# A mixture-of-experts kernel on one core: its expert blocks planned in two steps in place of three

## The chip, the core and the metric

The kernel runs on one core of one Trainium2 chip. The metric is the device time of one execution in microseconds (us). The core's engines are called as in the profile: PE (TensorE, the matmuls; PEld its weight loads), DVE (VectorE), ACT (ScalarE), POOL (GpSimd) and SP (SyncE, which here issues DMAs).

## What is computed

The input is x of 4 batches x 512 tokens x 256 features, all in fp32. Two residual layers follow each other; the layer norms in front of them have no parameters.

```python
x = x + attention(layernorm(x))
x = x + moe(layernorm(x))

def attention(x):                       # linear attention, 16 heads of 16
    q = k = elu(heads(x @ Wqk + bqk))
    v, u = silu(x @ Wv + bv), silu(x @ Wu + bu)
    out = merge(q @ (k^T @ v))          # per head
    return (u * layernorm(out, g, b)) @ Wo + bo

def moe(x):                             # 8 experts, the best 2 of each token
    top_w, top_i = top_k(x @ gate, 2)
    top_w = softmax(top_w)
    h = silu(x @ w0[e]) * (x @ w1[e])   # 256 -> 512
    return sum(top_w[e] * (h @ w2[e]) for e in top_i)   # 512 -> 256
```

There are 2048 tokens and two experts for each, so 4096 rows of expert work.

## The kernel before, in words

**Attention.** `attention(b)` is a generator that handles one batch in 15 stages, one for each `yield`. The loop over `at` runs the four batches staggered: batch b begins at `at` = 4b, and in each turn every batch that is under way does one stage. Stage 9 forms x1 (the first residual, matmuls `ap`) and writes it to the DRAM buffer `y` with a DMA from ACT. Stage 10 makes the third layer norm, `hn` (even quarters on DVE at L236, odd ones on ACT at L232). Stages 11 to 14 transpose it (`hTp`), multiply by the gate (`lp`), find the two best experts and each row's place (`mask`, `pre`, matmuls `pos`, `idx`), and scatter the rows with eight indirect DMAs from POOL (L461) into the DRAM buffer `xg`. There each expert has a region of its own, filled in the order of the tokens. A row carries its routing weight and the number of its token.

**Plans.** The expert work is cut into blocks of 128 rows of one expert. How many full blocks each expert has is known on the chip alone, so `plan(n, b)` works out a table of n blocks there: it sums the counts so far with a matmul (`tot`), and some 22 small DVE instructions turn them into a first row and two weight offsets for each block. `tot_False` and its tiles belong to plans of full blocks, `tot_True` to the last plan, whose blocks (names that end in r) may be partly empty. A number of full blocks is sure whatever the routing is: all rows so far, divided by 128, less 7 for what may be left over in eight experts.

**Blocks.** A block passes four functions, and `advance(block)` moves a new block in and each one in flight on by one:

- `fetch`: SP reads the first row from the table (L552) and issues a DMA of 128 rows of `xg` into a tile `g` (L567). There are 8 such tiles. Before the first r block, `pads()` writes empty rows behind each region's end, with eight DMAs on SP (L476), since partly empty blocks read past it.
- `turn`: PE transposes `g` into `gp` (L578), ACT copies it (L581), and then ACT and DVE each copy one half of the expert's first weights from `hw_sb` into a staging slot (L587).
- `hidden`: 32 matmuls `hp` (L598), silu into `s` on ACT (L604), a product `it` on DVE (L606).
- `finish`: 8 matmuls `eo` on w2 (L615), a scaling into `ys` on DVE (L620), and an indirect DMA from POOL that adds the rows to DRAM (L624). The rows go to `y`, or straight to the output for blocks in the list `held`, which run last; ahead of the first of those POOL copies all of `y` to the output (L623).

**Order.** When batches 1, 2 and 3 have gone through their last stage (at = 19, 23, 27), a plan is made of the blocks that are sure by then and were not planned yet: 9, 8 and 8. The first nine follow in `ready` after two empty turns (`[None] * 2`), one block for each turn of the loop. Of the eight of batch 2, five follow in `ready` and three are held back (`HELD = 3`). After batch 3 a second, last plan has 14 r blocks; eleven follow in `ready` and three run only where routing is that uneven (`rare`, under `tc.If`). At the end run the held blocks, the eight of batch 3 first. So the order is 9 and 5 blocks, 11 r blocks, 8 and 3 held ones, 36 in all. The instructions of each engine then run in the order that the built program gives them, which is close to that of the source; engines wait for each other by semaphores.

Of the kernel before, what the change touches and what calls it, by code (L numbers as in the profile page):

```python
# [19 lines left out]
P = 128  # L20
# [5 lines left out]
def kernel(  # L26
# [30 lines left out]
    B, N, E = x.shape  # L57
    NE, _, M = w0.shape
# [4 lines left out]
    T = B * N  # L63
    TOPK = 2
    BLOCKS = T * TOPK // P + NE - 1
    USUAL = T * TOPK // P + NE // 2
    HELD = 3
    REG = T + P
    ROW = E + 4
    HW = 2 * EC * M  # L70
# [407 lines left out]
    def plan(n, b, last=False):  # L478

        tot = psum.tile([P, NE], F32, tag="a", name=f"tot_{b}_{last}")
        nc.tensor.matmul(tot, lhsT=ones, rhs=state["count"], start=True, stop=True)
        vec = [1, NE]

        def tmp(shape, what):
            return small.tile(shape, F32, tag=what, name=f"{what}_{b}_{last}", bufs=1)

        c = tmp(vec, "c")
        nc.vector.tensor_copy(c, tot[0:1, :])  # L490
        if last:

            state["pads"] = const.tile(vec, I32, name="pads_at")
            nc.vector.tensor_tensor(state["pads"], c, region[0:1], ALU.add)
            nc.vector.tensor_scalar(c, c, float(P - 1), None, ALU.add)
        full = [1, NE, T // P]
        over = tmp(full, "over")
        nc.vector.tensor_tensor(
            over, c.unsqueeze(2).to_broadcast(full), ends, ALU.is_ge
        )  # L500
        new = tmp(vec, "new")
        nc.vector.tensor_reduce(new, over, AX.X, ALU.add)
        nc.vector.tensor_tensor(new, new, done, ALU.subtract)

        sq = tmp([1, NE, NE], "sq")
        nc.vector.tensor_tensor(
            sq, new.unsqueeze(1).to_broadcast([1, NE, NE]), upto[0:1], ALU.mult
        )
        cum = tmp(vec, "cum")
        nc.vector.tensor_reduce(cum, sq, AX.X, ALU.add)  # L510
        cumex = tmp(vec, "cumex")
        nc.vector.tensor_tensor(cumex, cum, new, ALU.subtract)

        base = tmp(vec, "base")
        nc.vector.tensor_tensor(base, done, cumex, ALU.subtract)
        nc.vector.scalar_tensor_tensor(base, base, float(P), region[0:1], ALU.mult, ALU.add)
        nc.vector.tensor_tensor(
            step[:, 0 : NE - 1], base[:, 1:NE], base[:, 0 : NE - 1], ALU.subtract
        )

        grid = [1, n, NE]
        behind = tmp(grid, "behind")
        nc.vector.tensor_tensor(
            behind, ordinal[:, 0:n, :], cum.unsqueeze(1).to_broadcast(grid), ALU.is_ge
        )
        which = tmp([1, n], "which")
        nc.vector.tensor_reduce(which, behind, AX.X, ALU.add)
        nc.vector.tensor_tensor(
            behind, behind, step.unsqueeze(1).to_broadcast(grid), ALU.mult
        )  # L530
        first = tmp([1, n], "first")
        nc.vector.tensor_reduce(first, behind, AX.X, ALU.add)
        nc.vector.scalar_tensor_tensor(
            first, first, base[:, 0:1], rows[:, 0:n], ALU.add, ALU.add
        )
        table = const.tile([1, 3, n], I32, name=f"table_{b}_{last}")
        nc.vector.tensor_scalar(table[:, 0, :], first, float(NE * REG), None, ALU.min)
        nc.vector.tensor_scalar(table[:, 1, :], which, float(NE - 1), float(HW), ALU.min, ALU.mult)
        nc.vector.tensor_scalar(table[:, 2, :], which, float(NE - 1), float(OW), ALU.min, ALU.mult)
        if last:  # L540
            state["rest"] = const.tile([1, 1], I32, name="rest")
            nc.vector.tensor_copy(state["rest"], cum[:, NE - 1 : NE])
        else:
            taken = tmp(vec, "taken")
            nc.vector.tensor_scalar(taken, cumex, -1.0, float(n), ALU.mult, ALU.add)
            nc.vector.scalar_tensor_tensor(taken, taken, 0.0, new, ALU.max, ALU.min)
            nc.vector.tensor_tensor(done, done, taken, ALU.add)
        return [(f"{b}_{j}{'r' if last else ''}", b, table[0:1, :, j : j + 1]) for j in range(n)]
# [11 lines left out]
    def fetch(block):  # L560

        j, b, entry = block
        if j == f"{B - 1}_0r":
            pads()
        row = read(entry[:, 0, :], NE * REG, mybir.EngineType.SP)
        g = blk.tile([P, ROW], F32, tag="g", name=f"g_{j}", bufs=8)
        ins = nc.sync.dma_start(out=g, in_=xg[bass.ds(row, P), :])  # L567
        tc.declare_no_dep(ins.ins, group=f"after {b}", reason="rows of batches up to b")
        tc.add_to_no_dep_group("reads", ins.ins)
        return block, g  # L570

    def turn(block, g):


        j, b, entry = block
        ps = psum.tile([P, EC, P], F32, tag="a", name=f"gp_{j}")
        for c in range(EC):
            nc.tensor.transpose(ps[:, c, :], g[:, bass.ts(c, P)], ident)  # L578
        gT = arena[:, 8, bass.ts(state["turned"] % 4, E)].rearrange("p (c n) -> p c n", c=EC)
        state["turned"] += 1  # L580
        nc.scalar.copy(gT, ps)  # L581
        at = read(entry[:, 1, :], (NE - 1) * HW, mybir.EngineType.Activation, mybir.EngineType.DVE)
        w = []
        for i, copy in enumerate((nc.scalar.copy, nc.vector.tensor_copy)):
            w.append(staging[state["staged"] % 4])
            state["staged"] += 1
            copy(w[i], hw_sb[:, bass.ds(at + i * EC * M, EC * M)])  # L587
        return block, w, g, gT

    def hidden(block, w, g, gT):  # L590

        j = block[0]
        both = []
        for i in range(2):
            ps = psum.tile([P, MC, P], F32, tag="a", name=f"hp_{j}_{i}")
            for m in range(MC):
                for k in range(EC):
                    nc.tensor.matmul(  # L598
                        ps[:, m, :], lhsT=w[i][:, bass.ds(k * M + m * P, P)],
                        rhs=gT[:, k, :], start=(k == 0), stop=(k == EC - 1),  # L600
                    )
            both.append(ps)
        s = work.tile([P, MC, P], F32, tag="s", name=f"s_{j}")
        nc.scalar.activation(s, both[0], AF.Silu)  # L604
        it = work.tile([P, MC, P], F32, tag="ex", name=f"it_{j}", bufs=4)
        nc.vector.tensor_tensor(it, s, both[1], ALU.mult)  # L606
        return block, g, it
# [26 lines left out]
    fetched, turned, made, held = [], [], [], []  # L634

    def advance(block=None):


        if block is not None:
            fetched.append(fetch(block))  # L640
        if fetched and (len(fetched) > 1 or block is None):
            turned.append(turn(*fetched.pop(0)))
        if turned and (len(turned) > 1 or not fetched):
            made.append(hidden(*turned.pop(0)))
        if made and (len(made) > 1 or not turned):
            finish(*made.pop(0))
# [3 lines left out]
    STAGES = 15  # L650
    W2_AT = 9
    begin = [0, 4, 8, 12]
    running = [attention(b) for b in range(B)]
    ready, ran, routed = [], 0, []
    for at in range(max(begin) + STAGES + 1):
        for b in range(B):
            if begin[b] <= at < begin[b] + STAGES:
                next(running[b], None)
        if at == begin[B - 1] + W2_AT:
            load_w2()  # L660

        b = begin.index(at - STAGES) if at - STAGES in begin else 0
        if b > 0:
            sure = -(-(b + 1) * N * TOPK // P) - NE + 1
            blocks = plan(sure - ran, b)
            ran = sure
            if b < B - 2:
                ready += [None] * 2 + blocks
            elif b < B - 1:
                ready += blocks[:-HELD]  # L670
                held += blocks[-HELD:]
            else:
                rest = plan(BLOCKS - ran, b, last=True)
                ready += rest[: USUAL - ran]
                rare = rest[USUAL - ran :]
                held = blocks + held
        if ready:
            block = ready.pop(0)
            if block:
                advance(block)  # L680
    for block in ready + held:
        advance(block)
    while fetched or turned or made:
# [62 lines left out]
```

## Time and profile before

| | us |
|---|---|
| median of 3 runs (354.87 to 356.56) | 356.35 |
| the profiled execution's own time | 355.68 |
| its span, first to last instruction | 353.6 |
| PE busy in the span | 307.8 |
| DVE, ACT, POOL busy | 175.3, 135.3, 120.8 |
| mean granted TensorE clock, of 1 | 0.947 |

A row of a timeline has the start and the length in us, the engine with its line, the operation, output<-inputs by the program's names without buffer numbers, and how many instructions were merged; in brackets, how long the engine had been idle before and what ended that. In the page's slices each digit is the busy share of 8.84 us in tenths. Attention and routing of all batches fill the first 152 us or so, with the first blocks among them; from then on blocks run alone.

### The profile page before, as it was taken

Reading aid. Unit: us, or ns where it says so; the run is one execution under the profiler, and the core shown is the slowest. Engines: PE = TensorE matmul, PEld = TensorE weight load, DVE = VectorE, ACT = ScalarE, POOL = GpSimd, SP = SyncE. Lnnn points to the kernel's source line nnn. Section 1 sums busy time; section 2 is a strip of 40 time slices with the busy share of each in tenths; the row PEclk is TensorE's granted clock in tenths of the full one; section 3 lists DMA queues with packets and bytes.
Section 4 is the critical chain, followed back from the end, with each engine's and each line's share of the span. In section 5 each row is a group of like instructions: output and inputs, shape, how many; then the busy total and the mean of one; then the engine's idle time right before and its main releaser. Section 6 shows DMA issues by size and latency. Waiting matters only on the chain. (4 is left out here: it accounts for less than half of the span.)

```text
span 353.6 us, 6144 instructions
## 1 busy us (share of the span) xinstructions
PE 307.8 (87%) x2048; PEld 274.4 (78%) x2048; DVE 175.3 (50%) x620; ACT 135.3 (38%) x204; POOL 120.8 (34%) x143
## 2 busy tenths in 40 slices
PE   0899899899767639995999999999999999999950
PEld 0467586777666439994999999999999999999940
DVE  4855879896694775663532323323233232342210
ACT  1455728647313135622323324333243332433200
POOL 5410211406617137266323324243242321333331
PEclk9999999999896678999999999999999999999995
DMA  7999012051364452143236332332323353332221
GB/s 216 369 386 373 9 59 62 1 179 66 115 184 173 121 154 92 15 92 90 46 57 157 62 47 45 59 47 48 47 46 60 47 166 120 60 48 30 32 32 15
DMA packets 27871, 35.58 MB, mean 101 GB/s; under 512 B 2848, under 2 KB 22688, under 8 KB 27808
## 3 DMA queue, kind: packets, MB, share of 16 engines
q1 hardware_dynamic: 18960, 22.00, 19.8%
q0 software_dynamic: 6768, 11.08, 17.2%
q10 hardware_dynamic: 2112, 2.10, 1.9%
q8 instruction: 18, 0.29, 0.3%
q14 instruction: 13, 0.11, 0.1%
HBM read 22.89 MB, written 14.37 MB: 105 GB/s over the span
## 5 line engine op out<-in xcount | busy, mean ns | idle before, releaser
L598 PE MATMUL hp<-arena 128*128 128x128 f32 x800 | 96.3, 280 | 4.1 <-ACT arena L587 4.1
L598 PEld LDWEIGHTS hp<-arena 128*128 128x128 f32 x800 | 94.2, 197 | 4.4 <-ACT arena L587 4.3
L606 DVE TENSOR_TENSOR it<-s,hp 128x512 f32<-128x512 f32 x25 | 17.2, 688 | 61.4 <-PE hp L598 52.7
L461 POOL DMA_INDIRECT xg<-hn,idx_i x32 | 32.4, 1012 | 43.8 <-DVE rs L228 34.5
L615 PE MATMUL eo<-arena,it 128*128 x200 | 47.1, 379 | 0.0
L624 POOL DMA_INDIRECT y<-ys,g x14 | 24.6, 1757 | 50.2 <-DVE ys L620 37.9
L615 PEld LDWEIGHTS eo<-arena,it 128*128 128x128 f32 x200 | 36.2, 190 | 3.9
L587 ACT COPY arena<-hw_sb 128x1024 f32 x36 | 37.6, 1045 | 2.9 <-ACT arena L581 0.8
L581 ACT COPY arena<-gp 128x256 f32<-128x256 f32 x25 | 9.3, 373 | 72.3 <-PE gp L578 68.6
L624 POOL DMA_INDIRECT out_dram<-ys,g x11 | 17.5, 1590 | 38.7 <-issue 17.8
L253 POOL TENSOR_TENSOR x<-x,bo 128x256 f32<-128x256 f32 x16 | 12.8, 824 | 40.9 <-DVE arena L236 32.5
L587 DVE COPY arena<-hw_sb 128x1024 f32 x36 | 25.0, 695 | 1.8 <-issue 0.8
L360 PE MATMUL ap<-wo,arena 128*128 128x256 f32 x64 | 18.4, 452 | 8.5 <-DVE arena L352 4.5
L360 PEld LDWEIGHTS ap<-wo,arena 128*128 128x128 f32 x64 | 14.3, 230 | 12.1 <-issue 4.3
L620 DVE TENSOR_SCALAR ys<-eo,g 128x256 f32<-128x256 f32 x25 | 12.1, 482 | 22.5 <-PE eo L615 22.5
L604 ACT ACTIVATE s<-hp 128x512 f32<-128x512 f32 x25 | 14.9, 597 | 19.6 <-PE hp L598 10.5
L265 PE MATMUL qp<-arena,wqk 128*128 128x512 f32 x32 | 16.4, 662 | 0.2 <-ACT arena L258 0.2
L283 PE MATMUL vp<-wv,arena 128*128 128x256 f32 x64 | 14.5, 379 | 0.0
L214 DVE BATCH_NORM_STATS2 st<-x 128x6 f32<-128x256 f32 x32 | 12.7, 415 | 3.5 <-DMA x<-in_x_dram 3.4
L297 PE MATMUL up<-arena,wu 128*128 128x512 f32 x32 | 14.4, 592 | 0.0
L283 PEld LDWEIGHTS vp<-wv,arena 128*128 128x128 f32 x64 | 12.0, 190 | 2.4 <-issue 1.0
L244 PE MATMUL xTp<-ident,arena 128*128 128x128 f32 x32 | 5.2, 311 | 9.9 <-DVE arena L236 9.9
(275 smaller groups left out, 488.7 us busy)
## 6 DMA issues: line engine op xcount, KB each, us to landing
hw_sb<-in_w_dram SPq DMA_DIRECT2D x16, 512.0 KB
arena<-in_w_dram SPq DMA_DIRECT2D x8, 512.0 KB
g<-xg SPq DMA_DIRECT2D x25, 130.0 KB
x<-in_x_dram SPq DMA_DIRECT2D x4, 512.0 KB
y<-x ACTq DMA_DIRECT2D x4, 512.0 KB
xg<-empty SPq DMA_DIRECT2D x9, 130.0 KB
xg<-hn,idx_i POOLq DMA_INDIRECT x32
wqk<-in_wqk_dram SPq DMA_DIRECT2D x1, 256.0 KB
```

The source lines that it names most:

```text
L253: nc.gpsimd.tensor_tensor(xb[:, t, :], xb[:, t, :], bo_sb, ALU.add)
L265: nc.tensor.matmul(ps, lhsT=wqk_sb[:, k, bass.ts(c, P)], rhs=xT[:, k, :], start=(k == 0), stop=(k == EC - 1),)
L283: nc.tensor.matmul(ps[:, t - t0, :], lhsT=xT[:, k, bass.ts(t, P)], rhs=wv_sb[:, k, :], start=(k == 0), stop=(k == EC - 1),)
L297: nc.tensor.matmul(ps, lhsT=wu_sb[:, k, bass.ts(c, P)], rhs=xT[:, k, :], start=(k == 0), stop=(k == EC - 1),)
L360: nc.tensor.matmul(ps[:, t - t0, :], lhsT=yT[:, c, bass.ts(t, P)], rhs=wo_sb[:, c, :], start=(c == 0), stop=(c == EC - 1),)
L461: apart(nc.gpsimd.indirect_dma_start(out=xg[:, :], out_offset=bass.IndirectOffsetOnAxis(ap=idx_i[:, t, k : k + 1], axis=0), in_=hn[:, t, k ...
L587: copy(w[i], hw_sb[:, bass.ds(at + i * EC * M, EC * M)])
L598: nc.tensor.matmul(ps[:, m, :], lhsT=w[i][:, bass.ds(k * M + m * P, P)], rhs=gT[:, k, :], start=(k == 0), stop=(k == EC - 1),)
L604: nc.scalar.activation(s, both[0], AF.Silu)
L606: nc.vector.tensor_tensor(it, s, both[1], ALU.mult)
L615: nc.tensor.matmul(ps, lhsT=it[:, m, :], rhs=w2_sb[:, bass.ds(at + m * E, E)], start=(m == 0), stop=(m == MC - 1),)
L624: ins = nc.gpsimd.indirect_dma_start(out=whole[:, :] if full else y[:, :], out_offset=bass.IndirectOffsetOnAxis(ap=g[:, E + 1 : E + 2].bit ...
```

## The change

One plan is made when batch 1 is through (nine blocks, as before), and none when batch 2 is. After the loop, behind batch 3, one plan takes all sixteen full blocks that are sure by then, and the last plan has its 14 r blocks as before. All sixteen are in `held`: they run last and add to the output. The first nine follow after one empty turn, not two. The order is 9 blocks, 11 r blocks, 16 held ones, again 36. The two plans behind batch 3 also stand after that turn's `advance`, no longer ahead of it.

```diff
-    HELD = 3
+    EARLY = 2 * N * TOPK // P - NE + 1
+    SURE = T * TOPK // P - NE + 1
...
-    ready, ran, routed = [], 0, []
+    ready = []
...
-        b = begin.index(at - STAGES) if at - STAGES in begin else 0
-        if b > 0:
-            sure = -(-(b + 1) * N * TOPK // P) - NE + 1
-            blocks = plan(sure - ran, b)
-            ran = sure
-            if b < B - 2:
-                ready += [None] * 2 + blocks
-            elif b < B - 1:
-                ready += blocks[:-HELD]
-                held += blocks[-HELD:]
-            else:
-                rest = plan(BLOCKS - ran, b, last=True)
-                ready += rest[: USUAL - ran]
-                rare = rest[USUAL - ran :]
-                held = blocks + held
+        if at == begin[1] + STAGES:
+            ready += [None] * 1 + plan(EARLY, 1)
         if ready:
             block = ready.pop(0)
             if block:
                 advance(block)
+
+    held += plan(SURE - EARLY, B - 1)
+    rest = plan(BLOCKS - SURE, B - 1, last=True)
+    ready += rest[: USUAL - SURE]
+    rare = rest[USUAL - SURE :]
     for block in ready + held:
         advance(block)
```

`EARLY` is 9 and `SURE` is 25.

## Prediction

> **What bounds the kernel now.** I read the page first (busy time, the slices, the chain that ended last), then the timeline of PE, then ACT and POOL where PE stood still.
>
> ```profile
> PE 307.8 (87%) x2048; PEld 274.4 (78%) x2048; DVE 175.3 (50%) x620; ACT 135.3 (38%) x204; POOL 120.8 (34%) x143
> PE   0899899899767639995999999999999999999950
> PEclk9999999999896678999999999999999999999995
> ```
>
> PE is the bound: 87% busy, and 9 in each slice of 8.84 us from 168 us on but the last two. The chain of waits holds only the last POOL adds (from 340.04 us), so the order of time decides the rest. The timeline of PE has no idle time from 166.71 us to its last matmul at 340.8 us; there a block costs 5.52 us (hidden layers start at 184.77, 190.29, 195.81). So a microsecond that PE wins or loses before 167 us arrives at the end. Timeline of PE (start, length, line, tiles, idle before it and what ended that):
>
> ```profile
> 124.04 0.41 PE L578 MATMUL gp<-ident,g 128*128 128x128 f32 x2
> 125.01 0.41 PE L433 MATMUL pos<-pre,ones 128*128 128x32 f32 x2 [0.56 <-DVE pre L427]
> 130.22 1.97 PE L244 MATMUL hTp<-ident,hn 128*128 128x128 f32 x8 [4.80 <-DVE hn L236]
> 131.98 0.43 PE L483 MATMUL tot_False<-pre,ones 128*128 128x8 f32 x2
> 132.26 0.67 PE L578 MATMUL gp<-ident,g 128*128 128x128 f32 x2
> 132.72 5.08 PE L598 MATMUL hp<-arena 128*128 128x128 f32 x32
> 137.64 1.85 PE L396 MATMUL lp<-gate,arena 128*128 128x8 f32 x16
> 139.34 0.42 PE L578 MATMUL gp<-ident,g 128*128 128x128 f32 x2
> 139.60 3.74 PE L598 MATMUL hp<-arena 128*128 128x128 f32 x32
> ...
> 162.26 0.38 PE L578 MATMUL gp<-ident,g 128*128 128x128 f32 x2
> 166.71 5.23 PE L598 MATMUL hp<-arena 128*128 128x128 f32 x32 [4.06 <-ACT arena L587]
> ```
>
> The reader is to see two holes in what PE has to do. The first, 4.80 us, waits for batch 3's third layernorm, while block 0 is already transposed (124.04). The second, 4.06 us, waits for a weight copy on ACT. After each, the 32 matmuls of a hidden layer take 5.08 and 5.23 us in place of 3.74. ACT, in both places:
>
> ```profile
> 124.49 0.37 ACT L581 COPY arena<-gp 128x256 f32<-128x256 f32 x1 [4.71 <-PE gp L578]
> 129.17 1.09 ACT L232 ACTIVATE hn<-x,nt,rs 128x256 f32<-128x256 f32 x2 [4.31 <-DVE nt L229]
> 130.16 1.03 ACT L587 COPY arena<-hw_sb 128x1024 f32 x1
> ...
> 157.16 0.37 ACT L581 COPY arena<-gp 128x256 f32<-128x256 f32 x1 [3.53 <-PE tot_True L483]
> 165.12 0.60 ACT L604 ACTIVATE s<-hp 128x512 f32<-128x512 f32 x1 [7.59 <-remote]
> 165.62 1.04 ACT L587 COPY arena<-hw_sb 128x1024 f32 x1
> ```
>
> At 130.16 block 0's weight copy stands behind hn on ACT, so PE had nothing for 4.8 us. At 165.12 the silu waited 7.59 us for matmuls that PE's rows have done by 158.9; "remote" says that the trace does not tell what released it. POOL wrote batch 3's eight scatters from 153.72 to 163.83; batch 1's ended at 114.06, and DVE, ACT, POOL and SP all moved again at 115.5 to 115.7. I read the second hole as PE's signals coming late while POOL scatters: a correlation of two cases, not a cause.
>
> [...] granted clock 0.50 in 128.70 to 135.50 and 0.51 in 166.20 to 169.70, 1.00 between. [...] first fetch issued 119.41, used at 124.04, so at most 4.6 us.
>
> **The change part by part.** Orders are those of the built program.
>
> 1. Block 0 goes one stage earlier (one None for two), and batch 2's plan is gone. On PE, block 0's 32 matmuls now stand before hTp of batch 3. On ACT, its weight copy goes ahead of the y write, and its table load (1.28) and first silu ahead of hn. Step by step: gp 123.8, its copy done 124.7, table read about 0.3, copies 1.03 (ACT) and 0.69 (DVE), so hp starts at 126.1 and takes 3.74 at full clock: 129.9. hn is delayed: DVE's even halves by the 0.69 copy to 130.5, ACT's odd halves by the silu to about 129.9; hTp runs 130.9 to 132.1, and the next hp starts at 132.5. Before, that one started at 139.60 with lp (1.70 from start to start) already behind it. Gain 139.60 - 1.70 - 132.5 = **5.4 us**, the removed tot (0.3) and the cold clock (5.08 - 3.74 = 1.3) within it. Batch 3's lp then stands at 137.9 for 137.64, its pos at 150.8 for 150.42: routing is 0.2 to 0.4 us later, not earlier.
> 2. Plan of batch 2 on DVE: 22 small instructions, 132.45 to 136.43. Worth nothing beyond part 1, for PE's hp (132.72) covered them. Batch 3's plan has rows of 16 for 8: 1x64 takes 0.20, 1x112 0.26, so three instructions grow by some 0.07, 0.2 us in the chain below.
> 3. The second hole. From hp at 132.5 PE goes on by 5.52 a block, 1.70 for lp and 0.4 for pos: hp of blocks 2 to 5 start at 139.7, 145.2, 151.2 and 156.7, tot at 162.0, hp of block 6 at 162.6. If no signal is late, the hole is gone: 4.06 + 1.49 cold = 5.5 gained. If they are late until 165 again, block 6's gp copy on ACT (due 156.7) comes at 165.1, its weight copy ends at 166.9 (0.37, 0.4, 1.03), and hp of block 6 starts there, not at 162.6: 4.3 + 1.5 cold = 5.8 lost. Both ends stay in the range. I take the late signals, since the eight scatters fall at 154 to 164 again (they follow pos). Net -0.3.
> 4. Cover of the last plan. Before, PE had seven blocks and more between tot (156.34) and the first rest block's gp (212.15). Now between tot (162.0) and gp_0r PE has hp 6, eo 5, hp 7, eo 6, both tot and two gp: 11.4 us. The chain: pads_at 1.7 after tot (158.03 for 156.34), its read about 0.6, eight pads and the wait for them 7.4 (SP: first pad 185.30, g_0r 192.66), [...] 14.3 with the fetch at its bound of 4.6. DVE's table for the rest stands behind block 6's product (`it`) and lies within that: hp 6 ends 166.3, table about 170. [...] with the late signals of part 3 PE comes 5.8 later, the pads at most 3. Taken at 0; the bound is 14.3 - 11.4 + 1.5 cold = 4.4. Nothing below 0 is to be had, since PE had no idle time there before.
> 5. SP loses five fetches ahead of the pads (they waited for g slots, so the pads started at 185.30) and gains five behind; 36 stay in all. POOL: five y adds become output adds. Those run one after another, 4.51 us apart (335.48, 340.04, 344.52), under PE's 5.52, so sixteen keep up as eleven did. The copy of y (8.9 us) has sixteen blocks to be caught up in. The last add starts 3.2 after the last ys before and after: 0. The number of blocks stays 36.
>
> Sum: 5.4 - 0.3 = **5.1 us** off. The profiled execution took 355.68 (span 353.6, 2.1 around it), 0.67 under the median of the runs: 350.6 on its own time, 351.3 on the median. Since part 3 is taken at its bad end, I say 350.5.
>
> **Rivals.**
> - No late signals: 5.4 + 5.5 = 10.9, less half at gp_0r: 346.0 on the median. For it: batch 2's scatters (128.44 to 138.92) held nothing for more than 0.6 us. Against: those of batches 1 and 3 did.
> - The signals come late in batch 2's scatters as well, where PE now has block work: hp of block 2 waits for its gp copy and lp for hT, 2.5 to 4 us plus 1.5 cold. That eats part 1: 355 to 356, no change. Also here: the earlier block 0 does not fill the hole, since something unseen holds its copies.
> - Slower: PE waits at gp_0r. In the profile of before the plan itself took 13.8 us from tot (156.34) to its last table write (170.20), the stall within it, and covered by spare blocks. If pads, scatters and fetch wait for each other on top, the chain decides from 11.4 us on. From 22.6 us it ends slower by half a percent (22.6 - 11.4 + 1.5 cold - 10.9 gained elsewhere = 1.8); at 25 us it gives 360.6. Against it: each part above was measured shorter.
>
> **Numbers.** Half a percent (1.8 us) is about what a measurement of this kernel can tell from no change. The likeliest case (late signals once) has 0.45, no late signals 0.30, no net change 0.13, slower by the chain 0.12. Faster: the first two and a little of the third, 0.79; same 0.10; slower 0.11. Range: 345.0 takes in most of the second case, 356.0 the third.
>
> **What would show it.** In the profile after: hp at about 126 us with idle under 1.5 us before it, and no 4.8 us before hTp; clock 1.00 from 122 to about 166. Right on part 3: a hole of about 4 us on PE before one hp at about 167, with ACT released at about 165. Right on part 4: gp_0r idle under 2 us. Wrong: a hole of over 4 us before gp_0r, hp of block 0 after 129 us, a late lp (over 140 us), or PE idle after 180 us.

## The result, and the profile after

The changed kernel takes 350.79 us (median of 4 runs, 349.07 to 351.27) beside 355.66 us before (a fourth run of that kernel, 354.97, moved its median from 356.35). The ratio is 0.9854, with a 95% interval of 0.9808 to 0.99: faster by 1.5%. The profiled execution took 350.45 us with a span of 348.3 us; that of before took 355.68 with 353.6.

From the page of the changed kernel: busy time of PE, its slices (8.7 us each) and the granted clock in the same slices.

```profile
PE 304.3 (87%) x2046; PEld 270.5 (78%) x2046; DVE 172.4 (50%) x599; ACT 134.5 (39%) x204; POOL 118.8 (34%) x143
PE   0899899899777579999689999999999999999950
PEclk9999999999896599999999999999999999999995
```

PE has the same share as before. The clock row shows what left: the 7 and 8 that before had at 124 to 141 us are 9 now, and only the dip at 104 to 122 us (6 and 5) stays, ahead of the change. A dent stays in PE's row at 165 to 183 us. The timeline of PE in the changed kernel (start, length, line, tiles, idle time before it and what ended that):

```profile
122.46 0.38 PE L579 MATMUL gp<-ident,g 128*128 128x128 f32 x2
124.77 3.84 PE L599 MATMUL hp<-arena 128*128 128x128 f32 x32 [0.30 <-ACT arena L588]
130.09 1.07 PE L245 MATMUL hTp<-ident,hn 128*128 128x128 f32 x8 [1.49 <-DVE hn L237]
...
131.39 3.84 PE L599 MATMUL hp<-arena 128*128 128x128 f32 x32
...
139.60 3.51 PE L599 MATMUL hp<-arena 128*128 128x128 f32 x30 [0.47 <-issue]
...
162.25 2.17 PE L599 MATMUL hp<-arena 128*128 128x128 f32 x18
164.95 0.51 PE L599 MATMUL hp<-arena 128*128 128x128 f32 x3 [0.52 <-issue]
166.36 1.40 PE L599 MATMUL hp<-arena 128*128 128x128 f32 x11 [0.91 <-issue]
...
173.72 2.02 PE L599 MATMUL hp<-arena 128*128 128x128 f32 x16 [2.23 <-DVE arena L588]
175.58 1.89 PE L616 MATMUL eo<-arena,it 128*128 x8
179.21 0.44 PE L579 MATMUL gp_0r<-ident,g_0r 128*128 128x128 f32 x2 [1.73 <-DMA g_0r<-xg]
```

Block 0's hidden layer now stands where PE had nothing to do, and hTp behind it waits 1.49 us in place of 4.80. The single hole of 4.06 us at 162 to 167 us, with its slow hidden layer, has become three smaller losses: hp of block 6 takes 5.34 us from its start to eo's (162.25 to 167.59) where an undisturbed one takes 3.57, its row broken by idle times marked "issue"; the second half of hp of block 7 waits 2.23 us for DVE's weight copy; and gp_0r waits 1.73 us for its fetch. A fourth, of some 0.6 us, is new in hp of block 2 (139.60), just behind POOL's scatters of batch 2 (128.19 to 138.34). ACT at the place of the old hole:

```profile
156.54 0.37 ACT L582 COPY arena<-gp 128x256 f32<-128x256 f32 x1 [3.14 <-PE gp L579]
159.23 0.60 ACT L605 ACTIVATE s<-hp 128x512 f32<-128x512 f32 x1 [1.16 <-PE hp L599]
166.54 0.37 ACT L582 COPY arena<-gp 128x256 f32<-128x256 f32 x1 [6.71 <-remote]
```

The last of these rows copies block 7's gp and starts 4.54 us behind the start of its transposes (162.00), which had ended at 162.41; ACT had been idle since 159.83, and "remote" names no cause. I call such a start late; the prediction's "late signals" are its reading of such starts, and the trace shows the starts alone. POOL's scatters of batch 3 (eight, one behind the other) run from 153.50 to 163.71. Within that burst not all is late: the copy at 156.54 follows its transposes (156.12) by 0.42 us, the silu at 159.23 its hp by 2.89, where the block before has 1.99.

### The profile page after: what moved, and what is told of

It reads as the page before. It is cut to its first block, busy times and chain, and to the rows that moved or that the text cites. A ratio compares the mean times of both kernels' runs of the same rounds, so it can differ in the third digit from the quotient of the medians.

```text
span 348.3 us, 6118 instructions
## 1 busy us (share of the span) xinstructions
PE 304.3 (87%) x2046; PEld 270.5 (78%) x2046; DVE 172.4 (50%) x599; ACT 134.5 (39%) x204; POOL 118.8 (34%) x143
## 5 line engine op out<-in xcount | busy, mean ns | idle before, releaser
L599 PE MATMUL hp<-arena 128*128 128x128 f32 x800 | 94.3, 275 | 4.4 <-DVE arena L588 2.2
L599 PEld LDWEIGHTS hp<-arena 128*128 128x128 f32 x800 | 91.8, 192 | 5.1 <-issue 4.6
L607 DVE TENSOR_TENSOR it<-s,hp 128x512 f32<-128x512 f32 x25 | 17.2, 687 | 64.7 <-PE hp L599 49.2
L625 POOL DMA_INDIRECT out_dram<-ys,g x16 | 26.3, 1644 | 57.4 <-issue 19.4
L625 POOL DMA_INDIRECT y<-ys,g x9 | 15.2, 1688 | 27.2 <-DVE ys L621 13.5
```

Source lines behind the costliest of these rows:

```text
L599: nc.tensor.matmul(ps[:, m, :], lhsT=w[i][:, bass.ds(k * M + m * P, P)], rhs=gT[:, k, :], start=(k == 0), stop=(k == EC - 1),)
L625: ins = nc.gpsimd.indirect_dma_start(out=whole[:, :] if full else y[:, :], out_offset=bass.IndirectOffsetOnAxis(ap=g[:, E + 1 : E + 2].bit ...
```

## The experiments

The twelve runs came in three sets of four, each on one chip, each set against the kernel before on the same chip. That kernel took 355.92, 359.35 and 343.31 us there, so a time is only read against its own set. Two rows of the table, before and changed, are the pair of the result above. What can be compared between sets, with one profile for each kernel, is the stretch of PE's timeline where the change acts. The table gives, in us, the start of the second hidden layer (hp of block 1), of the tenth, and what lies between, less 1.70 us where lp of batch 3 stands within it. From the tenth hidden layer to the end of the span every run needs 163.1 to 163.6 us (with eight more scatters 164.5), so nearly the whole difference is made ahead of it.

| kernel | second hp | tenth hp | between | ratio to before, 95% |
|---|---|---|---|---|
| before | 139.60 | 190.29 | 50.7 | 1 |
| changed | 131.39 | 185.00 | 51.9 | 0.9854 (0.9808 to 0.9900) |
| first set: e1_one_none | 131.55 | 189.52 | 56.3 | 0.9937 (0.9909 to 0.9964) |
| e2_two_none | 138.65 | 187.82 | 49.2 | 0.9895 (0.9851 to 0.9938) |
| e3_more_scatters | 133.08 | 194.75 | 60.0 | 1.0100 (1.0051 to 1.0150) |
| e4_cover | 130.87 | 182.61 | 50.0 | 0.9821 (0.9786 to 0.9857) |
| second set: e5_spaced | 127.61 | 181.42 | 52.1 | 0.9638 (0.9595 to 0.9681) |
| e6_plan_later | 133.37 | 190.29 | 55.2 | 0.9853 (0.9798 to 0.9908) |
| e7_later_spaced | 128.28 | 183.82 | 53.8 | 0.9720 (0.9674 to 0.9766) |
| e8_busy_pool | 128.48 | 182.50 | 52.3 | 0.9691 (0.9634 to 0.9747) |
| third set: after_again | 125.78 | 173.97 | 46.5 | 0.9919 (0.9889 to 0.9949) |
| e9_spaced | 126.71 | 179.18 | 50.8 | 1.0010 (0.9994 to 1.0027) |
| e10_behind | 126.36 | 173.16 | 45.1 | 0.9854 (0.9823 to 0.9885) |
| e11_pad_spaced | 126.15 | 178.39 | 50.5 | 1.0022 (1.0008 to 1.0037) |

**e1_one_none: the earlier block 0 alone.**

```diff
-                ready += [None] * 2 + blocks
+                ready += [None] * 1 + blocks
```

> The kernel before with one None in place of two ahead of the first plan's blocks: block 0 goes one stage earlier, and the three plans and the eleven held blocks stay. Theory (the earlier block 0 is the gain, and plans of 22 small DVE instructions cost nothing where they lie): the 4.80 us hole ahead of the third batch's hTp is gone, hp of block 0 starts at about 126, no clock of half speed at 128, and the time falls by about 5.4 us, to 350 beside 355.7. Between the last plan and the first r block lie the five blocks of the second plan, so gp_0r waits for nothing and the half of hp of block 7 that waited 2.23 us in the changed kernel doesn't: a further 2 to 4 us below the changed kernel is possible, 347 to 349. Rival (taking the middle plan out is what gained): the time stays at 354 to 356, and the hole is only moved.

Measured: 354.21 us beside 355.92, less than half of the gain. PE's timeline of this kernel:

```profile
131.16 0.29 PE L483 MATMUL tot_False<-pre,ones 128*128 128x8 f32 x2
131.55 3.84 PE L598 MATMUL hp<-arena 128*128 128x128 f32 x32
...
139.81 0.93 PE L396 MATMUL lp<-gate,arena 128*128 128x8 f32 x7 [0.93 <-issue]
140.85 5.36 PE L598 MATMUL hp<-arena 128*128 128x128 f32 x32
...
170.32 6.37 PE L598 MATMUL hp<-arena 128*128 128x128 f32 x32 [4.80 <-ACT arena L587]
```

The first hole is filled exactly as in the changed kernel (second hp at 131.55 beside 131.39), and 5.6 us more than in the kernel before are lost behind it. Some 3.7 of them are idle times in lp and a slow hp during batch 2's scatters (128.34 to 138.72) and just behind them; the other 1.9 come at batch 3's, where the hole is 4.80 us for 4.06 and the hp behind it 6.37 for 5.23. Here the middle plan's tot and DVE's 22 instructions lie in batch 2's burst. The time lies in the rival's range, not in the theory's; but the first hole is filled and not moved, and what is lost is lost at other places.

**e2_two_none: the changed kernel with block 0 at its old stage.**

```diff
-            ready += [None] * 1 + plan(EARLY, 1)
+            ready += [None] * 2 + plan(EARLY, 1)
```

> The changed kernel with two None ahead of the nine blocks, as before the change: one plan fewer, block 0 at its old stage. Theory (the earlier block 0 is the gain): the hole of about 4.8 us ahead of hTp of the last batch is back, with a clock of half speed behind it, and the time is 5 us above the changed kernel, 355 to 357; as the r blocks' cover shrinks by no block, the idle before gp_0r stays at about 2 us. Rival (the gain is the plan taken out, or the sixteen adds): 350 to 352, as the changed kernel.

Measured: 352.77 us, 3.2 below before. PE's timeline:

```profile
129.60 1.97 PE L245 MATMUL hTp<-ident,hn 128*128 128x128 f32 x8 [4.81 <-DVE hn L237]
...
172.97 2.02 PE L599 MATMUL hp<-arena 128*128 128x128 f32 x16 [2.34 <-DVE arena L588]
...
182.08 0.38 PE L579 MATMUL gp_0r<-ident,g_0r 128*128 128x128 f32 x2
```

The first hole is back with its slow hp (5.07 us from 131.78), as the theory said, but the time is not: without the middle plan, and with the last plans behind the advance, batch 3's burst costs less here (49.2 us between, for 50.7). And gp_0r waits for nothing, against the theory: with block 0 one stage later, three hidden layers stand between tot (160.92) and gp_0r, and in the changed kernel two. So the earlier block 0 uses up one block of cover, that is, of work that PE has while the plan and the fetch behind it are under way. Taken alone, block 0's place gives -0.6% (e1) and the rest of the change -1.05% (e2); their sum of 1.7% agrees, within the intervals, with the 1.5% of both.

**e3_more_scatters: eight scatters more.** Their destination is read by nothing.

```diff
+        if b == B - 1:
+            for t in range(NT):
+                for k in range(TOPK):
+                    ins = nc.gpsimd.indirect_dma_start(out=aside[:, :], ...)
```

> The changed kernel, with eight more indirect scatters behind the eight of the last batch: the same rows, written to a DRAM tensor that nothing reads. No block's fetch waits for them; on POOL the additions to y stand behind them. Theory (signals of PE reach the other engines late while POOL issues scatters): ACT's copy of gp_7, released at 166.5 in the changed kernel, is released at about 177, after the last extra scatter, or PE's hole of some 4 to 10 us appears between 162 and 178, and the time rises by 5 to 10 us, to 355 to 361. Rival (the lateness belongs to the program around that point and not to the scatters, or only to scatters that something waits for): ACT's copy is released within 1 us of 166.5, and the time stays within 1.5 us of the changed kernel's.

Measured: 360.36 us, 9.6 above the changed kernel's median. PE's timeline:

```profile
172.41 1.10 PE L610 MATMUL hp<-arena 128*128 128x128 f32 x4 [1.48 <-issue]
174.57 0.55 PE L610 MATMUL hp<-arena 128*128 128x128 f32 x1 [1.06 <-issue]
177.37 0.37 PE L610 MATMUL hp<-arena 128*128 128x128 f32 x1 [2.25 <-issue]
179.48 3.57 PE L627 MATMUL eo<-arena,it 128*128 x8 [1.74 <-remote]
```

ACT and POOL in the same run:

```profile
175.99 0.37 ACT L593 COPY arena<-gp 128x256 f32<-128x256 f32 x1 [15.06 <-issue]
```

```profile
174.75 0.97 POOL L471 DMA_INDIRECT aside<-hn,idx_i  x1 [0.30 <-issue]
```

The scatters, whose rows nothing reads, moved ACT's copy from 166.54 to 175.99, 0.3 us behind the last one's end (175.72) and 12.2 us behind its transposes (163.81); 1.8 us of the move are the burst's own later start in this run (155.30 for 153.50). PE's own matmuls creep as well, one to four between two idle times of 0.33 to 2.25 us, though the trace shows nothing that they wait for. The correlation of the prediction is a cause on this chip: with eight more scatters one behind the other, ACT's copy starts 9.45 us later and hp of block 6 takes 15.4 us from its start to eo's (164.06 to 179.48) in place of 5.34. What about the scatters does it stays open.

**e4_cover: three sure blocks ahead of the r blocks.**

```diff
-    held += plan(SURE - EARLY, B - 1)
+    sure = plan(SURE - EARLY, B - 1)
+    ready += sure[:3]
+    held += sure[3:]
```

> The changed kernel with the first three of the sixteen sure blocks run ahead of the r blocks, adding to y; thirteen stay at the end. Theory (the changed kernel's last plan is short of cover by 1.73 us at gp_0r): the fetch of the next block behind block 8 no longer stands behind the eight pads on SP, the idle of 1.73 us goes, and the time falls by 1.5 to 2 us, to about 349; the 2.23 us at the second half of hp of block 7 stays, since DVE's weight copy still stands behind both plans. Rival (that idle only moves: whatever PE waits there, it waits a block later): within 0.5 us of the changed kernel, 350.8.

Measured: 349.83 us. PE's timeline:

```profile
173.28 2.02 PE L599 MATMUL hp<-arena 128*128 128x128 f32 x16 [2.33 <-DVE arena L588]
...
193.43 0.38 PE L579 MATMUL gp_0r<-ident,g_0r 128*128 128x128 f32 x2
```

The idle time at gp_0r is gone and came nowhere else: 50.0 us between, for 51.9. The 2.33 us at block 7 stay, as expected. The trace shows the 1.9 us, the times about half of it, with an interval that overlaps that of the changed kernel: by the times alone a gain of e4 over it is not shown.

**e5_spaced, e7_later_spaced and e8_busy_pool: memsets on POOL.** They were to stand between the scatters of batch 3 (e5 on e4, e7 on e6), or behind them (e8 on the changed kernel).

```diff
+                if b == B - 1 and t + k > 0:
+                    for _ in range(6):
+                        nc.gpsimd.memset(spare, 0.0)
```

> The kernel with three sure blocks ahead of the r blocks, and in it six memsets of 128x128 on POOL between each two of the last batch's eight scatters, so that POOL issues scatters less than half of the time and the burst is some 18 to 20 us long in place of 10. Theory (signals of PE come late when POOL issues one scatter straight behind the other, and get through in the gaps): the late copy of gp_7 on ACT, the small 'issue' gaps of PE inside hp of block 6 (1.8 us) and the wait of 2.3 us at hp of block 7 are gone, and the time falls by 3 to 4 us, to 346 beside 349.8. Rival (signals are late for as long as a burst has not ended, however thin it is): as with the eight extra scatters, some 5 to 10 us slower, 355 to 360.

> As the one before (one None, three plans, the middle one two stages later), and the last batch's scatters spaced by six memsets each. Five blocks that need nothing of the last batch run behind the last plan, so that the longer burst is covered. Theory (late signals come with dense scatters): no hole above 1 us on PE from 145 to the end, clock 1.00, and the time is 5 to 7 us below that of the same kernel with dense scatters if its hole is the large one, 3 to 4 if the small one: 344 to 347. Rival (late as long as the burst lasts): a hole of 5 to 10 us, 354 to 360.

> The changed kernel with 48 memsets of 128x128 on POOL behind the last batch's eight scatters, so that POOL is busy for about as long as with eight more scatters but issues none. Theory (it is the issue of scatters that delays the signals, not a busy POOL): ACT's copy of gp_7 is released within 1 us of 166.5 and the time is within 1 us of the changed kernel's 350.8. Rival (a busy POOL is enough): as with the eight extra scatters, the release moves to about 174 and the time to 356 to 361.

Measured: 346.64, 349.69 and 348.37 us. None of the three tested what it was for: the memsets depend on nothing, and in the built program they stand in POOL's idle time at 5.7 to 29 us. The scatters are as dense as before and ACT starts as late (at 164.22 us in e8, 4.71 behind its transposes, with a burst that ends at 161.2). But all three had their second hp at 127.6 to 128.5 us, against 133.37 in the run of their set without memsets. What differs stands on POOL. In the changed kernel:

```profile
80.88 1.21 POOL L462 DMA_INDIRECT xg<-hn,idx_i  x1 [12.61 <-DVE rs L229]
```

In e8:

```profile
76.75 1.21 POOL L463 DMA_INDIRECT xg<-hn,idx_i  x1 [8.17 <-DVE mv L217]
```

Both wait for the weights in hn, written by 76.15 and 76.46. Without memsets the first scatter follows 4.7 us behind, with them 0.3. The DMA view of 76 to 80.8 us, for the changed kernel and then for e8, lists its queues (packets, MB, share of the 16 engines):

```profile
q1 hardware_dynamic: 653, 0.64, 40.1%
q8 instruction: 1, 0.02, 1.8%
q14 instruction: 1, 0.01, 0.4%
```

```profile
q1 hardware_dynamic: 699, 0.68, 42.0%
q0 software_dynamic: 96, 0.27, 15.1%
q8 instruction: 1, 0.02, 1.3%
```

A packet of the instruction queue q14 lies there in the kernel before, in the changed kernel on two chips and in e6, and in none of e5, e8 and e11, which have 42 or more POOL instructions added ahead. The packet and the first scatter's wait go together in these runs; that the one causes the other is not shown, for no run takes the packet away by other means. With it the burst starts 4 us later and falls on batch 1's attention: the second ap waits 3.42 us for DVE in e6, and 0.43 in e7, which differs from e6 by the memsets alone and is 5.1 us faster.

**e6_plan_later: the middle plan two stages later.** It takes batch 2's own counts, kept for it.

```diff
-        b = begin.index(at - STAGES) if at - STAGES in begin else 0
+        b = {19: 1, 25: 2, 27: 3}.get(at, 0)
```

> The kernel before with one None, and its middle plan two stages later, between the scatters of batch 2 and those of batch 3; three plans and eleven held blocks stay. Theory (the middle plan costs because its tot and 22 DVE instructions fall into the scatters of batch 2, where signals are late): the issue gaps of lp at 138 to 141 and the half clock behind them, about 3.6 us together, are gone, and the time is 350 to 351 beside 354.2 with the plan at its old place; whether the hole at 165 stays as 4.8 us or becomes the smaller one of the changed kernel depends on where the late signals catch ACT's queue, which makes 349 as well as 351 possible. Rival (a plan costs its time wherever it stands, or what was lost belongs to the held blocks): 353.5 to 355.

Measured: 354.83 us beside 359.35; between the hps 55.2 us, for 56.3 in e1. The two measures disagree. The ratio of 0.9853, with 0.9937 for e1, is what the theory's 350 to 351 us would give. But what the theory named is not in the trace: a loss at batch 2's burst stays (0.77 us idle, and a hp of 5.09), the hole at batch 3's stays too (5.52 us), and the stretch gives the plan's place about 1.1 us. Since e1 did not run on this chip, what the place is worth in time stays open; the theory's account of it is not borne out.

**after_again, e9_spaced, e10_behind and e11_pad_spaced: the third chip.** e9 puts between the scatters of e4 copies that cannot move; e11 is e9 with 48 memsets in addition; e10 is e1 with the two last plans behind the advance.

```diff
+                if b == B - 1 and t + k > 0:
+                    nc.gpsimd.tensor_copy(spare, hn[:, :, k, ROW - E : ROW])
```

> The changed kernel once more, on the same chip as the three runs beside it, so that they can be set against it: 0.985 of the kernel before, with the first scatter of POOL at about 80.9, 4.9 us behind the weights in hn, and the fetch of 8 KB of instructions ahead of it.

> The kernel with three sure blocks ahead of the r blocks, with a POOL copy of 128x1024 between each two of the last batch's eight scatters. The copies read the weights that the scatters wait for and so stay between them, which the memsets of the first attempt did not. POOL then issues a scatter every 2.5 to 3 us in place of 1.28, and the burst lasts some 20 us. Theory (signals of PE come late when POOL issues one scatter straight behind the other, and get through in the gaps): ACT's copy of gp_7 is released within 1 us of PE's transposes, PE's issue gaps inside hp of block 6 and the 2.3 us at hp of block 7 are gone, and the time is 3 to 4 us below that of the dense kernel, 0.972 of the kernel before in place of 0.982. Rival (signals are late for as long as a burst has not ended, however thin): the hole grows with the burst, as with eight more scatters, and the time is 5 to 10 us above, ratio 0.995 to 1.01.

> The kernel with one None and three plans, but the two plans of the last batch behind that turn's advance in place of ahead of it, where the changed kernel has them too: tot_False and tot_True stand behind hp of block 5 and eo of block 4 in place of ahead of them. Theory (the middle plan costs little, and what the changed kernel gained beyond the earlier block 0 comes from where the last plans stand: with the tots ahead, ACT's Silu of block 5 falls behind the moment from which signals are late, and ACT's queue then holds the next block's copies): the hole of 4.8 us at 165 and the half clock behind it become the 4 us of the changed kernel, and the time is 3 us below the same kernel with the plans ahead, 0.984 to 0.987 of the kernel before in place of 0.994. Rival (it is the number of plans or of held blocks that costs): 0.992 to 0.996.

> The spaced kernel with 48 memsets of 128x128 on POOL in addition, which stand in POOL's idle time of the first 30 us, as in the three kernels where memsets went there unintended. Theory (they shift the place in POOL's program at which it has to fetch instructions, so that the first scatter starts at 76.5 in place of 80.9 and the second ap waits 0.4 us in place of 3.4): 3 to 5 us below the spaced kernel, 0.960 to 0.965 of the kernel before if the spacing works, and below 0.975 if it does nothing. Rival (those three were faster for the chip or the layout in SBUF): no faster than the spaced kernel, first scatter at about 80.9.

Measured: 339.76, 343.84, 338.81 and 344.30 us, beside 343.31 of before. The changed kernel is 0.8% below before here, not the 1.5% expected; its first scatter (80.30, 4.6 us behind the weights) and the packet on q14 ahead of it are about as expected. On this chip ACT did not start late in batch 3's burst. PE and ACT of the changed kernel on it:

```profile
155.77 0.42 PE L579 MATMUL gp<-ident,g 128*128 128x128 f32 x2
156.03 3.74 PE L599 MATMUL hp<-arena 128*128 128x128 f32 x32
...
168.17 0.44 PE L579 MATMUL gp_0r<-ident,g_0r 128*128 128x128 f32 x2 [1.16 <-DMA g_0r<-xg]
```

```profile
156.22 0.37 ACT L582 COPY arena<-gp 128x256 f32<-128x256 f32 x1 [3.54 <-PE gp L579]
```

ACT follows gp by 0.45 us although the scatters run from 147.26 to 157.49. So the late starts belong to the chip (or to its state at the time) together with the scatters, and no spacing could gain here: e9 and e10 could not tell apart what they were made for. The same program's span is 11.2 us shorter here than in the first profile (337.1 for 348.3): 5.6 us ahead of the second hp, where ap of batch 3 starts at 110.91 for 117.20, and 5.4 between the two marks of the table.

The runs tell two other things. e10 has the earlier block 0, the middle plan and full cover, and loses nothing at all in the stretch (45.1 us). It is faster than both kernels there: than before by 1.5%, than the changed kernel by 0.3% (medians) to 0.7% (ratios, whose intervals just miss each other). So, where ACT does not start late, the middle plan is free, and what the changed kernel is short of is cover at gp_0r.

And e9 paid for its copies. DVE, then POOL, in e9:

```profile
157.74 1.73 DVE L507 TENSOR_TENSOR new_False<-new_False,done 1x8 f32<-1x8 f32 x1
```

```profile
158.40 1.04 POOL L464 COPY spare<-hn 128x1024 f32<-128x1024 f32 x1
```

A DVE instruction on 8 elements takes 1.73 us for 0.15 in the changed kernel on this chip, and ends as POOL's copy does. Three such instructions (1.59 to 1.73 us) end within 0.04 us of a copy's end; their rows begin 0.5 to 0.7 us before the copy's, while the scatter ahead of it is on POOL. What held them the trace does not show. With these three in the last plans, the half of hp of block 7 waited 3.80 us for DVE. e11's first scatter stood at 75.86 us as its theory said, but the time did not fall. On this chip the earlier burst had nothing to gain: PE's idle time ahead of all its ap rows is 4.0 us in the changed kernel here, for 8.3 on the first chip, with its first scatter at 80.30.

## Why the prediction was right, and where its steps were not

The time and the sum held: 350.5 us said and 350.79 measured; 5.1 us predicted, 4.87 between the medians and 5.23 between the profiled executions. Step 1, the largest term, held in its mechanism. That the sum came so near is in part luck: the loss of step 3 was put too high and that of step 4 too low, and the two errors (1.8 and 1.7 us) nearly cancel; and 0.75 us of the 5.23 are a head start that the change did not make.

- **Step 1, block 0 (5.4 us).** Measured 139.60 - 1.70 - 131.39 = 6.5, of which 0.75 is that head start, from before the change takes effect (ap of batch 3 at 117.20 for 117.95; in the first set it starts anywhere from 116.19 to 118.54): 5.8. The cold window behind it is gone: the granted clock is 1.00 in 124 to 140 us. e2 shows the hole back when block 0 is put back, and on the third chip e10, which fills the hole and loses nothing behind it, is 4.5 us below before (it has the last plans at their new place too). Right in mechanism and size.
- **Step 2, the middle plan is worth nothing.** Right on the third chip (e10). On the first, keeping it and the last plans' old place cost e1 some 3 us against the changed kernel (0.9937 for 0.9854); the step looked at what covered the plan at its old place, not at what it would meet once block work stood in batch 2's burst. How much of the 3 us is the plan's place e6 leaves open. Whether the rest belongs to the last plans, which e1 and e6 have ahead of the advance so that a Silu on ACT falls among the late starts, stays open too: e10 was made for that, and ran where ACT did not start late.
- **Step 3, late signals once more (net -0.3).** That late starts would recur was right (4.54 us at block 7's copy), and e3 shows the scatters as their cause on that chip. The step put the delay on block 6's gp copy, a hole of 4.3 us with 1.5 us of slow clock. That copy was in time (156.54), block 7's was late, and PE lost 1.8 us in creeping matmuls and 2.23 us behind DVE; no cold clock followed (granted 1.00 in 140 to 180 us). The term of 5.8 us lost was 4.0. The 0.6 us at block 2 is a small part of what the second rival put at batch 2's burst.
- **Step 4, cover (0, bound 4.4).** gp_0r waited 1.73 us, inside the bound. On the third chip, where ACT did not start late, it still waits 1.16. The step named the right chain, the pads; that its cost was 0 was the author's estimate, for the trace of before bounds the time of the fetch (4.6 us) and does not show it. Up to the fetch the step had 9.7 us (1.7, 0.6 and 7.4), a little too short: on the third chip the first pad is issued 2.25 us behind tot_True (155.54) and g_0r's fetch 7.95 us behind the first pad, 10.2 in all. gp_0r starts 2.43 us behind the fetch: 12.6 us, and PE has work for 11.5 of them. What SP waited for ahead of that fetch (in all, times, longest):

```profile
SPq L568 <- DMA xg<-empty: 1.4, 1, 1.4
SPq L553 <- DVE table_True L538: 1.1, 1, 1.1
```

SP first waits for the table of the r blocks (written at 163.75) and reads it, and then for the pads to land. In e10 the table is written by 164.34, long before the first pad at 172.85, and there SP waits 2.8 us for the pads, and the fetch comes 7.78 us behind the first of them all the same. So the wait for the pads ends last, with that for the table close ahead of it. On the first chip, with the late starts, the first pad comes 4.6 us later (the step: at most 3) and PE's arrival 4.2 us later (the step: 5.8), and so the wait is 1.73 there.

- **Steps 3 and 4 together** cost 1.2 us more than the hole they replaced (51.9 for 50.7 between) where 0.3 was said. With 5.8 and the head start of 0.75 that gives 5.3, the difference of the spans.
- **Step 5, SP and POOL (0).** Right: from the tenth hidden layer to the end 163.3 us before and after. The step's 8.9 us for the copy of y are a wait on POOL in the trace of before: its first add into the output stands idle 8.86 us, ended by that copy.

Of the signs that the prediction had set, those for the earlier block 0 and for gp_0r came; the hole of about 4 us ahead of one hp, its sign for step 3, did not.

The rival without late signals came true on another chip (ACT 0.45 us behind gp there), where the change gives 3.6 us by the medians (2.8 by the ratio) and not 10. The kernel before was not profiled there. At 343.31 us it can hardly have had the second hole to lose: e10 fills the first hole and loses nothing behind it, and is 4.5 us faster, less than step 1 alone gave on the first chip.

## What to carry to other kernels

A hole that is filled gives its time only if what follows does not meet the next wait sooner: read a schedule change as "how far ahead is PE here" and "what does it lose from here on", at two fixed marks of the timeline. The cover that a plan needs is counted along all that stands between it and the first use of its blocks, here the table, the pads' landing and the fetch; 12.6 us of such a chain over 11.5 us of cover cost 1.16 us of idle time. In a burst of indirect DMAs from POOL, one copy on ACT, which waits for none of them, started 4.5 to 4.7 us behind PE's transposes on two of the three chips here (the changed kernel, e8), and 0.45 behind them on the third; measure on more than one chip before trusting a gain of one percent.

## What the runs showed of the hardware

- With scatters back to back on POOL (one each 1.28 us), the ACT row that reads PE's results started late, 0.3 to 3 us past the burst's end (1.3 in the kernel before, 2.8 in the changed one, 0.3 in e3, 3.0 in e8), and PE's matmuls stood between idle times of 0.3 to 2.3 us; eight more scatters moved that row by 9.5 us, 1.8 of them by the burst's later start. On another chip the changed kernel showed none of it in batch 3's burst (0.45 us from gp to ACT's copy), and the kernel before took 343.31 us there for 355.92 and 359.35. What differs between the chips is not known.
- POOL's first scatter stood 4.7 us behind its operands, with one packet of the instruction queue q14 in between; with 48 POOL instructions added earlier (e8) no such packet was there and the scatter started 0.3 us behind them.
- Beside POOL copies of 1.04 us, three DVE instructions of 0.15 us took 1.59 to 1.73 us and ended with the copies.
